# Squares of 32 by 32, loaded by DMA and turned by VectorE, in place of TensorE's transpositions with an identity

## The chip, the core and the metric

The kernel runs on one core of one Trainium2 chip. The metric is the device time of one execution in microseconds (us). The core has five engines that work side by side, each through its own list of instructions in order: TensorE (PE in the profile; PEld are its weight loads), VectorE (DVE), ScalarE (ACT), GpSimd (POOL) and SyncE (SP), which here only issues transfers. Transfers (DMAs) are issued by SP and by ScalarE and are carried out by 16 DMA engines. A DMA is cut into pieces that are contiguous in memory on both sides; the profile calls them packets.

## The reference, cut to what matters

Eight graphs (B = 8) of N = 2048 nodes with F = 256 features pass through two layers. Layer 0 is attention with 4 heads of 64 over chunks of 256 keys, each with a softmax of its own; layer 1 is graph attention with a score that is a sum of a source and a target term.

```python
# layer 0
q, k, v = (x @ W.T + b).reshape(B, N, 4, 64).transpose(0, 2, 1, 3)   # for Wq, Wk, Wv
scores = einsum('bhnd,bhjcd->bhnjc', q, kc) / 8       # keys in 8 chunks of 256
scores = where(mask == 0, -10, clip(scores, -10, 10))
attn = softmax(scores, axis=-1)                       # inside each chunk
ctx = einsum('bhnjc,bhjcd->bhnd', attn, vc)           # summed over the chunks
o = ctx.reshape(B, N, 256) @ Wo.T + bo + x
o = layernorm(o) * gamma + beta
x1 = layernorm(x + o)
# layer 1
Wh = x1 @ W1                                          # 4 heads of 64
e = leaky_relu(s_src[i] + s_dst[j], 0.2)              # s = einsum(Wh, a)
alpha = softmax(where(adj, e, -inf)); h = elu(alpha @ Wh)
out = layernorm(x1 + h)
```

A matrix product on TensorE contracts over the 128 partitions. So x, the contexts and x1, which come with nodes on the partitions, must be turned (features on the partitions) before they are multiplied with a weight matrix. That turning is what the change is about.

## The kernel before, in words

Everything is float32. The nodes of a graph are cut into four blocks of CH = 512 (index g or q); a block is QT = 4 tiles of 128 nodes. qT and kT hold queries and keys turned (128 features of a head pair by nodes, KC = 2 such halves); vaug holds the values with a column of ones, so that a product gives the softmax's sums too.

A graph's layer 0 is a loop over 64 slots (`for s in range(SLOTS)`, L837): four query blocks q, two head pairs hp, eight key chunks c; i = s % 16 is the slot's place within its query block. In a slot TensorE computes the scores of the next slot (`scores`, L335), VectorE clips and masks them (L346), ScalarE takes exponentials (L358), TensorE multiplies with the values (`product`, L368, in two halves k), ScalarE copies the result out of PSUM (L375), VectorE inverts the sums and GpSimd adds the chunk to the context (`normalize`, L383 to L392). Between the two halves of `product` stands a part of layer 1 of the graph before: three tiles, for each of which VectorE makes edge factors (L651) and TensorE multiplies (L671). In the first graph the masks are turned there instead (class `Masks`). So two graphs are always in work: layer 0 of b and layer 1 of b - 1.

Three things are turned by TensorE, as a product with an identity into PSUM, then copied to SBUF by ScalarE:

- x for the projections: `transposed` (L252), eight transpositions of 128 by 128 (L258) and a copy (L261). `project(b, g)` gives the pieces load, turn, keys, values, queries of a block.
- the contexts: `context(q, hp)` (L394), four transpositions (L399) and a copy into qT (L402), whose old queries are used up by then. It runs for hp = 0 at the end of slot 9 and for hp = 1 at the end of slot 1 of the next query block.
- x1: `Between.turn(c)` (L493), four transpositions (L498) and a copy (L501) for each half c. `Between` takes a finished query block through the output product (L466), residual, two norms, and the product with W1 (`values`, L514). Its steps are spread over the slots of the next query block by two tables: BESIDE (ahead of the slot's products, on VectorE) and BEHIND (after them).

Within each engine the order is the program's (`manual_schedule`); nothing is reordered. Transfers are issued by SP in program order too, each when what it waits for is done: masks for the clip three slots ahead (`load_slab`, L322), edges eight tiles ahead (L633), x blocks (L247). x1 is also kept in DRAM (x1D) for the residual of layer 1; the store goes to a list `outgoing` that SP works off at the top of a slot. Small buffers of a pool with one tag share its count of buffers: "xb" (two) serves x to be projected, x as residual and x1 as residual, "xT" (two) serves all turned blocks.

Between the slots of two graphs stands a list `order` (L910): the last query block's `Between`, whose x1 is turned by `transposed` (`turn_all`), the four projections of the next graph, and the factors of layer 1. After the last graph layer 1 runs alone.

Of the kernel before, what the change touches and what calls it, by code (L numbers as in the profile page):

```python
# [17 lines left out]
P = 128  # L18
CH = 512
# [3 lines left out]
def adj_resnorm_kernel(  # L23
# [37 lines left out]

    QS = HP * NK
# [45 lines left out]
    x1D = tc.dram_tile([B, NCH, P, QT, F], F32, name="x1D")  # L108
# [135 lines left out]

    def load_x(b, g, name):
        t = blocks.tile([P, QT, F], F32, tag="xb", name=name)
        nc.sync.dma_start(  # L247
            out=t, in_=x[b, g * CH : (g + 1) * CH, :].rearrange("(t p) f -> p t f", p=P)
        )
        return t  # L250

# [12 lines left out]
    def project(b, g):  # L264
# [4 lines left out]
        def load():  # L269
            st["x"] = load_x(b, g, "xp")  # L270

        def turn():
            st["xT"] = transposed(st["x"], "xT")
# [119 lines left out]

    def context(q, hp):  # L394

# [44 lines left out]
    class Between:  # L440
# [48 lines left out]
        def finish(self):  # L489
            self.b2.apply(self.y)  # L490
            outgoing.append(lambda: nc.sync.dma_start(out=x1D[self.b, self.g], in_=self.y))

        def turn(self, c):  # L493
            if c == 0:
                self.x1T = blocks.tile([P, KC, CH], F32, tag="xT", name="x1T")
            pt = psM.tile([P, CH], F32, tag="psM", name="pt")
            for k in range(QT):
                nc.tensor.transpose(  # L498
                    pt[:, k * P : (k + 1) * P], self.y[:, k, c * P : (c + 1) * P], identf
                )  # L500
            nc.scalar.copy(self.x1T[:, c, :], pt)  # L501
# [29 lines left out]

    BESIDE = {
        1: [lambda o: o.bias()],
        3: [lambda o: o.add((0, 1))],
        4: [lambda o: o.add((2, 3)), lambda o: o.a.stats((0, 1))],
        5: [lambda o: o.a.stats((2, 3)), lambda o: o.shift()],
        7: [lambda o: o.scale()],
        8: [lambda o: o.again(), lambda o: o.b2.stats((0, 1))],
        9: [lambda o: o.b2.stats((2, 3))],
    }  # L540
    BEHIND = {
        2: lambda o: o.output((0, 1)),
        3: lambda o: o.output((2, 3)),
        6: lambda o: o.a.apply(o.y),
        10: lambda o: o.finish(),
        11: lambda o: o.turn(0),
        12: lambda o: o.turn(1),
        13: lambda o: o.values((0,)),
        14: lambda o: o.values((1,)),
        15: lambda o: o.values((2,)),  # L550
    }

# [169 lines left out]
    class Close:  # L722


        def __init__(self, b, g):
# [3 lines left out]
            nc.sync.dma_start(out=self.x, in_=x1D[b, g])  # L729
# [5 lines left out]
        def finish(self):  # L735
            o = blocks.tile([P, QT, F], F32, tag="y", name="o")
            self.n.apply(o)
            rows = slice(self.g * CH, (self.g + 1) * CH)
            outgoing.append(
                lambda: nc.sync.dma_start(  # L740
                    out=out[self.b, rows, :].rearrange("(t p) f -> p t f", p=P), in_=o
                )
            )
# [77 lines left out]
    for b in range(B):  # L821
# [15 lines left out]
        for s in range(SLOTS):  # L837
# [5 lines left out]
            before = group  # L843
            if i == 0:
                group = Between(b, q - 1, sd, waug) if q else None
            if s:
                normalize(s - 1)
            if s + 1 < SLOTS:
                scores(s + 1)

            if group:
# [15 lines left out]
            if i == 0 and before:  # L867
                before.values((3,))
            if i == 1 and q:
                context(q - 1, 1)  # L870
            if i == QS // 2 + 1:
                context(q, 0)
# [33 lines left out]
        if b + 1 < B:  # L906
            (l0, t0, k0, v0, q0), (l1, t1, k1, v1, q1), (l2, t2, k2, v2, q2), (l3, t3, k3, v3, q3) = [
                project(b + 1, g) for g in range(NCH)
            ]
            order = [l0, begin, lambda: before.values((3,)), steps[0], t0, k0, ctx, l1, v0, steps[1]]  # L910
# [72 lines left out]
```

## Time and profile before

Three runs took 3926.72, 3927.82 and 3929.75 us. The profiled execution took 3929.08 us, with a span of 3927.3 us and a mean granted TensorE clock of 0.993.

| what | profile | where |
|---|---|---|
| turning x on TensorE | 256 transpositions, 34.1 us busy | L258 |
| turning contexts on TensorE | 256, 41.6 us busy | L399 |
| turning x1 on TensorE, in slots | 192, 31.5 us busy | L498 |
| turning x1 on TensorE, last block of a graph | 64, 9.6 us busy | L258 |
| copies behind them on ScalarE | 1012 ns for 1024 columns, 607 to 611 ns for 512 | L261, L402, L501 |
| scores, clip, exponentials in slots | 1022.7 us PE, 1192.6 us DVE, 1051.4 us ACT | L335, L346, L358 |
| products of layers 0 and 1 | 1159.6 and 1088.8 us PE | L368, L671 |
| edge factors | 1343.2 us DVE | L651 |

How to read it: "busy" is the time in which at least one instruction of a group ran, so matmuls that overlap are not counted twice, and the mean of one instruction (here about 275 ns for a transposition) is longer than its share of the busy time. In a line of the timeline the first number is the start in us, the second the length of a run of like instructions, then engine, line, operation, the tile written and those read, and the count; a bracket gives idle time ahead of it and what ended it. A view of waits or of one engine's timeline shows more of the limit than the shares do, because stages differ: the first graph has no layer 1 beside it, and the last layer 1 has no layer 0.

### The profile page before, as it was taken

The page shows a single profiled execution, that of the slowest core. Times are in us where ns is not written, and L with a number is a line of the kernel's source. Part 1 is how long each engine was busy: PE and PEld are TensorE (multiplying, and loading weights), DVE is VectorE, ACT ScalarE, POOL GpSimd, SP SyncE. Part 2 cuts the span into 40 slices and gives each one's busy share as a digit, 9 for nine tenths or more (in the row PEclk, how much of TensorE's full clock was granted, in tenths as well). Part 3 has the DMA queues.
Part 4 walks back from the last instruction along what each step waited for, and adds up shares of the span by engine and source line. Part 5 has one row for each costly group of instructions (what it writes and reads, how often), then busy time and mean ns, then how long its engine had stood idle before and what let it go on. Part 6 is the DMA issues. An engine that isn't in the chain of part 4 may idle for free. (4 is left out here: it accounts for less than half of the span.)

```text
span 3927.3 us, 160298 instructions
## 1 busy us (share of the span) xinstructions
PE 3781.5 (96%) x72740; PEld 2820.0 (72%) x72740; DVE 3115.4 (79%) x4698; ACT 2028.6 (52%) x3753; POOL 1388.4 (35%) x1202
## 2 busy tenths in 40 slices
PE   7998999999999999999999999999999999999787
PEld 4665677776777767776777767777677776776676
DVE  3776398885988769885898849888598876987798
ACT  4665445554555555555555545555455555555321
POOL 0444233332343333432443324433243333434310
PEclk9999999999999999999999999999999999999899
DMA  6641232222322233331432224322232323322244
GB/s 150 136 93 35 70 92 80 83 72 93 105 84 85 63 115 91 85 85 59 128 92 81 81 75 122 84 78 72 93 108 81 85 63 115 95 80 71 84 144 124
DMA packets 379259, 356.50 MB, mean 91 GB/s; under 512 B 87376, under 2 KB 335568, under 8 KB 378576
## 3 DMA queue, kind: packets, MB, share of 16 engines
q1 hardware_dynamic: 375040, 344.02, 30.5%
q8 instruction: 568, 9.31, 1.0%
q10 hardware_dynamic: 3536, 2.23, 0.2%
q14 instruction: 115, 0.94, 0.1%
HBM read 303.96 MB, written 42.21 MB: 88 GB/s over the span
## 5 line engine op out<-in xcount | busy, mean ns | idle before, releaser
L346 DVE SCALAR_TENSOR_TENSOR pr<-ps,slab 128x1024 f32<-128x1024 f32 x1024 | 1192.6, 1205 | 284.3 <-PE ps L335 283.5
L368 PEld LDWEIGHTS pc<-vaug,pr 128*64 128x64 f32 x32768 | 1041.1, 138 | 437.5 <-issue 248.4
L651 DVE SCALAR_TENSOR_TENSOR e<-srow,gd,et 128x640 f32<-128x640 f32 (+1 forms) x1536 | 1343.2, 930 | 6.2 <-PE pa L671 6.2
L368 PE MATMUL pc<-vaug,pr 128*64 128x65 f32 x32768 | 1159.6, 224 | 37.3 <-ACT raw L375 31.9
L358 ACT ACTIVATE pr<-pr 128x1024 f32<-128x1024 f32 x1024 | 1051.4, 1056 | 229.4 <-DVE pr L346 212.7
L671 PE MATMUL pa<-waug,e 128*64 128x65 f32 x32768 | 1088.8, 224 | 41.0 <-DVE e L651 37.5
L671 PEld LDWEIGHTS pa<-waug,e 128*64 128x64 f32 x32768 | 1023.4, 139 | 71.1 <-DVE e L651 37.4
L335 PE MATMUL ps<-qT,kT 64*128 64x512 f32 x4096 | 1022.7, 617 | 11.0 <-DVE pr L346 8.1
L390 POOL TENSOR_TENSOR part<-raw,rd 128x512 f32<-128x512 f32 x448 | 468.6, 1046 | 1442.3 <-DVE rd L383 1425.2
L375 ACT COPY raw<-pc 128x260 f32<-128x260 f32 x1024 | 382.1, 373 | 1129.2 <-PE pc L368 1111.9
L335 PEld LDWEIGHTS ps<-qT,kT 64*128 64x128 f32 x4096 | 352.7, 186 | 345.6 <-issue 223.4
L392 POOL TENSOR_TENSOR acc<-acc,part 128x512 f32<-128x512 f32 x448 | 574.2, 1282 | 35.2
L383 DVE RECIPROCAL rd<-raw 128x8 f32<-128x8 f32 x512 | 101.1, 197 | 172.5 <-ACT raw L375 165.6
L390 POOL TENSOR_TENSOR acc<-raw,rd 128x512 f32<-128x512 f32 x64 | 66.8, 1043 | 387.4 <-DVE rd L383 386.6
L699 ACT ACTIVATE hh<-pa,dn 128x64 f32<-128x64 f32 x512 | 114.2, 321 | 100.7 <-DVE dn L695 96.9
L514 PE MATMUL pw<-w_sb,x1T 128*128 128x264 f32 x512 | 141.3, 406 | 4.3 <-ACT sd L525 4.3
L279 PE MATMUL pp<-xT,wk_sb 128*128 128x512 f32 x256 | 120.1, 613 | 18.6 <-ACT xT L261 18.1
L426 POOL TENSOR_TENSOR rs_c<-rs_c,nhalf 128x4 f32<-128x4 f32 x32 | 55.6, 1737 | 226.8 <-DVE off_c L425 226.8
L466 PE MATMUL po<-wo_sb,qT 128*128 128x256 f32 x512 | 124.8, 389 | 0.0
L279 PE MATMUL pp<-xT,wq_sb 128*128 128x512 f32 x256 | 117.5, 602 | 5.5 <-DVE y L477 3.1
L295 PE MATMUL pv<-wv_sb,xT 128*128 128x256 f32 x512 | 115.9, 379 | 0.0
L426 POOL TENSOR_TENSOR rs_a<-rs_a,nhalf 128x4 f32<-128x4 f32 x32 | 56.3, 1761 | 153.2 <-DVE off_a L425 153.2
(93 smaller groups left out, 2050.7 us busy)
## 6 DMA issues: line engine op xcount, KB each, us to landing
et<-edgeD SPq DMA_DIRECT2D x256, 320.0 KB, 3.1
slab<-clipD SPq DMA_DIRECT2D x512, 128.0 KB, 3.4
et<-edgeD SPq DMA_DIRECT2D x128, 384.0 KB, 3.6
srow<-rowD SPq DMA_DIRECT2D x64, 320.0 KB, 4.4
xp<-in_x_dram SPq DMA_DIRECT2D x32, 512.0 KB, 4.5
xg<-in_x_dram SPq DMA_DIRECT2D x32, 512.0 KB, 4.9
x1D<-y SPq DMA_DIRECT2D x32, 512.0 KB, 3.0
x1g<-x1D SPq DMA_DIRECT2D x32, 512.0 KB, 5.5
```

The costliest lines, as they stand in the source:

```text
L279: nc.tensor.matmul(pp[:, c, :], lhsT=w[:, kc, c * P : (c + 1) * P], rhs=st["xT"][:, kc, :], start=(kc == 0), stop=(kc == KC - 1),)
L335: nc.tensor.matmul(ps[:, k, :], lhsT=kT[rows, hp, t * P : (t + 1) * P], rhs=qT[rows, hp, cols], start=True, stop=True,)
L346: nc.vector.scalar_tensor_tensor(pr, pss[u], -CLIP, slab[:, u, :].unsqueeze(1).to_broadcast([P, 2, CH]), op0=ALU.max, op1=ALU.min,)
L358: nc.scalar.activation(pr, pr, AF.Exp, scale=0.125)
L368: nc.tensor.matmul(pc[z * D : (z + 1) * D, i, :], lhsT=probs[s][u][:, k, i * P + z * D : i * P + (z + 1) * D], rhs=vaug[:, KT * c + u, 2 * ...
L375: nc.scalar.copy(raws[s][:, k], pc)
L390: nc.gpsimd.tensor_mul(part, raw[:, :, :, :D], rd.to_broadcast([P, 2, QT, D]))
L392: nc.gpsimd.tensor_add(accv, accv, part)
L466: nc.tensor.matmul(po[:, k, :], lhsT=qT[:, c, t * P : (t + 1) * P], rhs=wo_sb[:, c, :], start=(c == 0), stop=(c == KC - 1),)
L514: nc.tensor.matmul(pw[:, k, : F + 2 * H], lhsT=self.x1T[:, c, u * P : (u + 1) * P], rhs=w1_sb[:, c, :], start=(c == 0), stop=(c == KC - 1),)
L651: nc.vector.scalar_tensor_tensor(e[:, :w], self.rows[n][:, :w], self.gd[:, h, j : j + 1], self.edge[k // JG][:, j % JG, :w], op0=ALU.max, ...
L671: nc.tensor.matmul(self.pa[z * D : (z + 1) * D, i * D1 : (i + 1) * D1], lhsT=e[:, i * P + z * D : i * P + (z + 1) * D], rhs=self.waug[:, j ...
```

## The change

Each of the three is turned in another way, except the last query block of each graph, which is left as it was (its hp = 1 context and its x1).

A block that lies in DRAM with a node per row is loaded by `load_squares`: for each 32 features one DMA puts, for all groups of 32 nodes, node r of the group on partition a * 32 + r, and the 32 features of it (128 B) next to those of the other groups. So each square of 32 nodes by 32 features stands in its final place, but unturned. VectorE's transpose then turns every square of 32 by 32 in place of its grid, and the whole is turned. A block of x or x1 takes eight such DMAs with 512 pieces each and one VectorE instruction of 1024 columns; a context half takes four DMAs and 512 columns.

- x is in DRAM already. Block 0 of the next graph is now loaded at the top of slot 63, ahead of `order`; the turn of block 0 stands right behind `begin`.
- A context is first stored to a new DRAM array ctxD, by a DMA on ScalarE's queue at the end of slots 0 and 8 (`send_context`), is loaded at the top of slots 1 and 9, after the slab's load (`load_context`), and turned in slots 3 and 11, behind the clip (`turn_context`), straight into qT.
- x1 is stored, now as rows by node, on ScalarE's queue behind the last norm (slot 11); it is loaded back at the top of slot 12 and turned in slot 14. x1D's new layout also holds for the residual of layer 1.

The steps of `Between` move by a slot to the later side, and the four `values` pieces move to the ends of slots 14 and 15 and of slots 0 and 1 of the next query block (table AFTER). For the query block before the last, the second pair of `values` falls into `order`.

```diff
+    def load_squares(dst, src):
+        for c in range(src.shape[1] // P):
+            for a in range(P // SQ):
+                f0 = c * P + a * SQ
+                nc.sync.dma_start(
+                    out=dst[a * SQ : (a + 1) * SQ, c, :].rearrange("r (k s) -> r k s", s=SQ),
+                    in_=src[:, f0 : f0 + SQ].rearrange("(k r) s -> r k s", r=SQ),
+                )
+    def turned(t, name):
+        dst = blocks.tile([P, KC, CH], F32, tag="xT", name=name)
+        nc.vector.transpose(dst.rearrange("p c n -> p (c n)"), t.rearrange("p c n -> p (c n)"))
+        return dst
...
-            st["x"] = load_x(b, g, "xp")
+            st["x"] = load_turned(x, b, g, "xp")
-            st["xT"] = transposed(st["x"], "xT")
+            st["xT"] = turned(st["x"], "xT")
...
+    def send_context(b, q, hp):
+        acc = accs.pop((q, hp))
+        cols = slice(hp * P, (hp + 1) * P)
+        nc.scalar.dma_start(
+            out=by_node(ctxD, b, q)[:, :, cols], in_=acc.rearrange("p t k d -> p t (k d)")
+        )
+    def load_context(b, q, hp):
+        t = small.tile([P, 1, CH], F32, tag="ctx", name="ctx", bufs=1)
+        load_squares(t, ctxD[b, q * CH : (q + 1) * CH, hp * P : (hp + 1) * P])
+        sums[q, hp] = t
+    def turn_context(q, hp):
+        nc.vector.transpose(qT[:, hp, q * CH : (q + 1) * CH], sums.pop((q, hp))[:, 0, :])
...
-            outgoing.append(lambda: nc.sync.dma_start(out=x1D[self.b, self.g], in_=self.y))
+            nc.scalar.dma_start(out=by_node(x1D, self.b, self.g), in_=self.y)
+        def load(self):
+            self.t = load_turned(x1D, self.b, self.g, "x1t")
+        def turn(self):
+            self.x1T = turned(self.t, "x1T")
...
+    AHEAD = {12: lambda o: o.load()}
     BESIDE = {
         1: [lambda o: o.bias()],
-        3: [lambda o: o.add((0, 1))],
-        4: [lambda o: o.add((2, 3)), lambda o: o.a.stats((0, 1))],
-        5: [lambda o: o.a.stats((2, 3)), lambda o: o.shift()],
-        7: [lambda o: o.scale()],
-        8: [lambda o: o.again(), lambda o: o.b2.stats((0, 1))],
-        9: [lambda o: o.b2.stats((2, 3))],
+        4: [lambda o: o.add((0, 1))],
+        5: [lambda o: o.add((2, 3)), lambda o: o.a.stats((0, 1))],
+        6: [lambda o: o.a.stats((2, 3)), lambda o: o.shift()],
+        8: [lambda o: o.scale()],
+        9: [lambda o: o.again(), lambda o: o.b2.stats((0, 1))],
+        10: [lambda o: o.b2.stats((2, 3))],
+        14: [lambda o: o.turn()],
     }
     BEHIND = {
-        2: lambda o: o.output((0, 1)),
-        3: lambda o: o.output((2, 3)),
-        6: lambda o: o.a.apply(o.y),
-        10: lambda o: o.finish(),
-        11: lambda o: o.turn(0),
-        12: lambda o: o.turn(1),
-        13: lambda o: o.values((0,)),
-        14: lambda o: o.values((1,)),
-        15: lambda o: o.values((2,)),
+        3: lambda o: o.output((0, 1)),
+        4: lambda o: o.output((2, 3)),
+        7: lambda o: o.a.apply(o.y),
+        11: lambda o: o.finish(),
+        14: lambda o: o.values((0,)),
+        15: lambda o: o.values((1,)),
     }
+    AFTER = {0: lambda o: o.values((2,)), 1: lambda o: o.values((3,))}
...
+            if i == 1 and q:
+                load_context(b, q - 1, 1)
+            if i == QS // 2 + 1:
+                load_context(b, q, 0)
+            if group and i in AHEAD:
+                AHEAD[i](group)
+            if s == SLOTS - 1 and b + 1 < B:
+                turns = [project(b + 1, g) for g in range(NCH)]
+                turns[0].pop(0)()
...
-            order = [l0, begin, lambda: before.values((3,)), steps[0], t0, k0, ctx, l1, v0, steps[1]]
+            order = [begin, t0, lambda: before.values((2, 3)), steps[0], k0, ctx, l1, v0, steps[1]]
```

## The prediction

> **What bounds the kernel now**
>
> I read the engines' busy shares first, then the work in order of time inside single slots, then the groups by shape, and last the transfers. (The chain that ended last covers only the final microseconds here and says nothing about the rest.)
>
> ```profile
> PE 3781.5 (96%) x72740; PEld 2820.0 (72%) x72740; DVE 3115.4 (79%) x4698; ACT 2028.6 (52%) x3753; POOL 1388.4 (35%) x1202
> ```
>
> A busy PE need not be the bound, so I take two neighbouring slots of the second batch (TensorE, in order of time; start, length):
>
> ```profile
> 629.79 1.99 PE L335 MATMUL ps<-qT,kT 64*128 64x512 f32 x8
> 631.71 1.15 PE L368 MATMUL pc<-vaug,pr 128*64 128x65 f32 x32
> 632.69 1.92 PE L671 MATMUL pa<-waug,e 128*64 128x65 f32 x60
> 634.44 1.10 PE L368 MATMUL pc<-vaug,pr 128*64 128x65 f32 x32
> 635.48 1.99 PE L335 MATMUL ps<-qT,kT 64*128 64x512 f32 x8
> ...
> 640.12 1.10 PE L368 MATMUL pc<-vaug,pr 128*64 128x65 f32 x32
> 641.16 0.66 PE L399 MATMUL pt<-identf,acc 128*128 128x128 f32 x4
> 641.75 1.99 PE L335 MATMUL ps<-qT,kT 64*128 64x512 f32 x8
> ```
>
> Without extras a slot takes 635.48 - 629.79 = 5.69 us; with one context's four transposes 641.75 - 635.48 = 6.27 us, and no wait stands between. TensorE sets the slot, and four transposes cost it 0.58 us.
>
> VectorE is the next limit. The same stretch on it:
>
> ```profile
> 632.26 2.30 DVE L346 SCALAR_TENSOR_TENSOR pr<-ps,slab 128x1024 f32<-128x1024 f32 x2
> 634.48 1.48 DVE L486 TENSOR_TENSOR y<-y,xg 128x1024 f32<-128x1024 f32 x1
> 636.00 0.75 DVE L416 BATCH_NORM_STATS2 st_b<-y 128x6 f32<-128x256 f32 x2
> 639.37 2.31 DVE L346 SCALAR_TENSOR_TENSOR pr<-ps,slab 128x1024 f32<-128x1024 f32 x2
> ```
>
> Undisturbed, the clip (L346) starts 1.18 us after the slot's scores begin (607.77 after 606.59). Here it starts at 639.37 instead of 635.48 + 1.18, so VectorE runs 2.7 us behind. One group later this lag reaches 3.0 us, and the slot takes 6.50 us instead of 6.27. A lag of 2.8 us is therefore about what the slots absorb.
>
> Between two batches TensorE also waits for the copy out of PSUM that each transposition needs:
>
> ```profile
> 883.64 1.04 PE L258 MATMUL pt<-identf,xp 128*128 128x128 f32 x8
> 885.78 3.70 PE L279 MATMUL pp<-xT,wk_sb 128*128 128x512 f32 x8 [1.10 <-ACT xT L261]
> 896.66 1.04 PE L258 MATMUL pt<-identf,xp 128*128 128x128 f32 x8
> 898.14 0.70 PE L279 MATMUL pp<-xT,wq_sb 128*128 128x512 f32 x1 [0.44 <-DVE y L477]
> ```
>
> [...]
>
> - [...] row L451 has 1214 ns. I price a turn alike: estimate 1.2 us for 1024 columns, 0.65 us for 512.
> - [...]
> - [...] The new loads move pieces of 128 B.
>
> The trace can price such a piece. From 30 to 75 us, where masks are stored in 128 B pieces, the transfers show:
>
> ```profile
> DMA packets 19792, 7.72 MB, mean 172 GB/s; under 512 B 17014, under 2 KB 18175, under 8 KB 19789
> q1 hardware_dynamic: 19789, 7.68, 80.1%
> ```
>
> 0.801 x 45 us x 16 engines / 19789 is 29 ns per packet over all. Taking off the 2775 large ones, estimated at 50 ns (1161 of 1 KB; the page's mean on q1 is 0.305 x 3927 x 16 / 375040 = 51 ns) and 150 ns (1614, by their bytes), leaves 277 us for 17014: 16 ns. But these are stores; small loads from scattered DRAM rows are not shown. Bounds: 7 ns (128 of the mean 917 B at 51 ns) and 51 ns (a piece costs a mean packet). I take 15 ns.
>
> **The change part by part, against the profiled span of 3927.3 us**
>
> *Contexts and x1 inside slots.* A batch has seven contexts in slots (0, 0; then two each for q = 1, 2, 3, less the last, which stays on TensorE) and six x1 half blocks (three groups of two). Each takes 0.59 us of TensorE: row L399 gives 41.6 us / 256 x 4 = 0.65, less overlap. So 13 x 0.59 = 7.7 us per batch, 61 us in eight. The first batch has no second-layer work but shows the same 0.58 (394.17, 399.43). Projected values only move a slot later; one more of them falls between batches and one less into a slot: nothing. ScalarE loses its copies, which were off the path.
>
> *What VectorE pays.* It gains 2 x 0.65 + 1.2 = 2.5 us per group of 16 slots. Measured start to start, its own slot is 4.7 us, 0.98 under TensorE's 5.68. The added values reach slot 14 (turn of x1), where TensorE has 6.77 us: hidden. The turn in slot 3 stands beside an output product (7.6 us): hidden. The turn in slot 11 does not stand in such company. The norm's steps are one slot later, and slots 9 to 12 have lost transposes that gave VectorE time. Lag, slot by slot: 0.5 at slot 6; 7.3 us of work, 2.15 at slot 7; 1.2; 1.6; again, statistics and L707 (7.6 us), 3.5 at slot 10. That is 0.7 beyond 2.8, then 0.2 at 11 and 0.1 at 12: 1.0 us of stall, against 0.3 now. Loss 0.7 us per group, 21 groups with a second layer beside them: 15 us.
>
> *The transfers.* A context is stored from ScalarE's queue at the end of slots 0 and 8, its squares are loaded in the next slot, and needed two slots after that: 15.8 us after the load's slot begins, against about 2.5 (store) + 1.6 (four issues) + 3 = 7. Hidden. For x1 it is tight. Now the apply runs to 3.9 us after its next slot's start (1581.40 + 2.08 against 1579.57). Add the store, 4.1 us (as for the output, which has the new layout):
>
> ```profile
> out_dram<-o SPq DMA_DIRECT2D x32, 512.0 KB, 4.1
> clipD<-clip SPq DMA_DIRECT2D x32, 80.0 KB, 2.0
> xp<-in_x_dram SPq DMA_DIRECT2D x32, 512.0 KB, 4.5
> ```
>
> so loads start 8.0 us into slot 12. They are eight issues of 0.39 us (the median of today's x issue, which also has 512 pieces) with 256 pieces per engine: the larger of 3.1 and 256 x 15 ns = 3.8, plus 2.2 to land, 6.0 us. x1T is needed by TensorE at 3 x 5.68 = 17.0, less 1.2 for the turn: 15.8. Ready at 14.0, so 1.8 us spare. SP stands still meanwhile until slot 12 + 11 us. Behind it are slabs (three slots ahead) and edge chunks (eight tiles, 15 us ahead), so nothing starves. ScalarE's queue waits at a store for GpSimd's sum, which ends about 2.3 us into the slot, earlier than the copy ahead of the store, and for the eighth transfer before it in the program (eight completion counters go round), which is some slots old; the exponentials behind it are not held. On VectorE, the edge factors (L651) and the next clip stand behind a turn, so a late load reaches TensorE through both. In the first batch slots are 4.7 us and the spare vanishes: loss 1 us.
>
> *Between batches*, seven times. x0 is loaded a slot ahead and turned while TensorE does other work: 1.04 + 1.10 = 2.1 us. Turn 3: 1.04. Turns 1 and 2 go too (1.48 + 1.27), but TensorE then meets the norm of the last group: 16.3 us from the end of its output product (896.7 to 913.0), with 14.5 us of products left in front of the turn instead of 17.3. Gain there 1.0. Sum 4.1 us, 29 us in seven. The next x waits only for VectorE's turn, 7 us to load against 12 us between turns.
>
> *Start.* The first product waits until 15.67 us for ScalarE, which is held by weight loads. VectorE turns x at about 11: 4 us gained. The phase's transfers go from 80% towards 95%, so I keep 4.
>
> Sum: 61 - 15 - 1 + 29 + 4 = 78 us, 3849 on the profiled span; its run took 3929.1 and the others 3926.7 to 3929.8, so 3849 for the median.
>
> **Rivals**
>
> *VectorE takes it back.* If it absorbs no more than now, each group in slots loses its gain of 2.4 us rather than 0.7: another 21 x 1.7 = 36 us, 3885. For: VectorE's share in 490 to 866 us is 337.5 / 376 = 90%. Against: slots 13 to 3 show no lag, and the larger turn lies there. A turn at double price adds 0.65 at slot 11, 14 us.
>
> *x1's load is late.* At 30 ns a piece the load takes 2.5 + 7.7 = 10.2 us, ready at 18.2, 2.4 late, in 24 groups: 58 us less gain, 3907.
>
> *Slower.* The same place at 51 ns: 2.5 + 13.1 = 15.6 us, 7.8 late, 187 us, so 4036. The gain is gone when each of the 24 loads is 78 / 24 = 3.3 us late, at 34 ns a piece. For: unmeasured scattered reads. Against: 16 ns for the stores.
>
> *The transposes were hidden anyway.* Then no change; the slot above speaks against it (6.27 to 5.69).
>
> **How the numbers follow**
>
> Main case 0.66 (3815 to 3875: from no added stall, no loss at the norm, up to double-price turns); VectorE 0.14 (3885); late load 0.08 (3907); slower 0.09; no change 0.03. The range 3815 to 3893 holds the first two. 0.2% is about what the runs can tell apart. Faster 0.88, same 0.03, slower 0.09.
>
> **What would show it**
>
> Slots with a context at 5.7 us, not 6.27; no wait of TensorE between first turn and L279; VectorE's transposes at 1.2 and 0.65 us; a clip lag up to 3.5 us at slot 10. Wrong, if VectorE waits for x1t or ctx transfers in slots 14, 3 or 11, if TensorE waits for x1T, or if TensorE's slots stay as long although the transposes are gone.

## The result, and the profile after

The changed kernel takes 3890.01 us, median of 4 runs (3888.07 to 3892.72); the kernel before, on the same chip, 3928.49 us (3926.72 to 3929.75). The ratio is 0.9903, 95% interval 0.9886 to 0.992. It is faster by 38.5 us, half of the 79 us forecast. The profiled execution spans 3888.7 us against 3927.3 us, 38.6 us less, so the two traces can be compared directly.

The first line of the page that answers to the one shown of before:

```profile
PE 3696.5 (95%) x72068; PEld 2752.5 (71%) x72068; DVE 3204.7 (82%) x4810; ACT 1946.2 (50%) x3601; POOL 1384.4 (36%) x1202
```

TensorE lost 85 us of busy time and 672 instructions, VectorE gained 89 us. But the span fell by only 39 us: TensorE now waits more. The view of TensorE's waits names where (total us, how often, longest), first of after, then of before:

```profile
PE pc L393 <- ACT raw L400: 63.1, 104, 2.3
```

```profile
PE pc L368 <- ACT raw L375: 31.9, 56, 1.9
```

The attention product (`product`, L393) waits for ScalarE's copy of the product before it out of PSUM (`raw`, L400). This wait doubled, although ScalarE's own load fell. Of the added 31 us, 21.7 lie in slots 8 and 13 of the second to fourth groups of 16 slots (in batches with a second layer), where the kernel before has none of these waits, and 6.2 in slot 13 of the first group.

To see what it is, here are two neighbouring slots of the second batch, in order of time (start, length, and in brackets a wait with its releaser). TensorE, from slot 12 of a group to slot 14:

```profile
747.59 1.99 PE L360 MATMUL ps<-qT,kT 64*128 64x512 f32 x8
...
753.55 1.99 PE L360 MATMUL ps<-qT,kT 64*128 64x512 f32 x8
756.22 1.15 PE L393 MATMUL pc<-vaug,pr 128*64 128x65 f32 x32 [0.68 <-ACT raw L400]
...
759.98 1.99 PE L360 MATMUL ps<-qT,kT 64*128 64x512 f32 x8
```

VectorE and ScalarE at the same time:

```profile
751.49 2.30 DVE L371 SCALAR_TENSOR_TENSOR pr<-ps,slab 128x1024 f32<-128x1024 f32 x2
```

```profile
752.69 2.19 ACT L383 ACTIVATE pr<-pr 128x1024 f32<-128x1024 f32 x2 [0.28 <-DVE pr L371]
754.79 1.11 ACT L737 ACTIVATE hh<-pa,dn 128x64 f32<-128x64 f32 x5
755.77 0.40 ACT L400 COPY raw<-pc 128x260 f32<-128x260 f32 x1
```

Read them from the bottom. TensorE could have started L393 at 755.54 and starts at 756.22, when the copy of `raw` is done. The copy was ready to go when the second product of slot 12 ended, but ScalarE works in order: the exponentials came first, and after them `hh`, five activations of the second layer's tail, 1.11 us. The exponentials were late because the clip (L371) started at 751.49, which is 751.49 - 747.59 - 1.18 = 2.72 us behind. Slot 13 takes 759.98 - 753.55 = 6.43 us instead of 5.68. The lag alone, 2.72 us, is within the 2.8 us that the forecast allowed. With `hh` in its way it is not.

Between two batches, VectorE and then TensorE, at the second gap and (last line) at the third:

```profile
874.97 0.49 DVE L745 SCALAR_TENSOR_TENSOR h<-ee,hp 128x320 f32<-128x320 f32 x1 [2.50 <-ACT hp L743]
875.38 1.24 DVE L274 STREAM_TRANSPOSE xT<-xp 128x1024 f32<-128x1024 f32 x1
```

```profile
876.67 5.40 PE L304 MATMUL pp<-xT,wk_sb 128*128 128x512 f32 x8 [2.32 <-DVE xT L274]
...
1339.29 3.70 PE L304 MATMUL pp<-xT,wk_sb 128*128 128x512 f32 x8 [2.32 <-DVE xT L274]
```

VectorE had x0 in SBUF and nothing else to do, yet its turn starts at 875.38: in program order it stands behind L745, the end of the last tail, and that waits for ScalarE. TensorE waits 2.32 us, twice the 1.10 us of before. In the second gap the same eight products then take 5.40 us instead of 3.70; the granted clock was 0.77 from 877 to 879 us and 0.58 from 879 to 882 us.

The transfers, which the forecast doubted most, from the page and from the lists of single instructions (min/median/max ns):

```profile
xp<-in_x_dram SPq DMA_DIRECT2D x256, 64.0 KB, 2.3
```

```profile
L435 DVE STREAM_TRANSPOSE qT<-ctx x56: 695/702/707, 138.5 to 3604.1; 128x512 f32<-128x512 f32 x56
```

A transfer of 64 KB, sixteen squares, lands in 2.3 us. In the trace's record of single packets one of 128 B takes 12.9 ns of a transfer engine in the mean (409,600 of them); in the kernel before, where the 65,536 packets of this size are all stores, it takes 12.9 ns too. The lists show no wait of VectorE for a context or for x1 in the slots with a second layer.

**Where the 38.6 us are.** I took the start of every slot's scores from the trace. A gap is the time from the last scores of a batch to the first of the next. One product of projected values, 6.77 - 5.68 = 1.09 us, moved per batch from the slots into the gap (in the last batch, into the end); the third column has it put back.

| part | measured | without the moved product | forecast |
|---|---|---|---|
| slots, 8 batches | 3084.3 to 3055.0: -29.3 | -20.6 | -61 + 16 = -45 |
| gaps, 7 | 495.6 to 486.7: -9.0 | -16.6 | -29 |
| start | +0.3 | +0.3 | -4 |
| end | -0.6 | -1.7 | 0 |
| sum | -38.6 | -38.6 | -78 |

So 24 us are missing in the slots, 12 in the gaps and 4 at the start.

### The profile page after: what moved, and what is told of

Same layout as the page of the kernel before. It is cut to its first block, busy times and chain, and to the rows that moved or that the text cites. A ratio compares the mean times of both kernels' runs of the same rounds, so it can differ in the third digit from the quotient of the medians.

```text
span 3888.7 us, 160154 instructions
## 1 busy us (share of the span) xinstructions
PE 3696.5 (95%) x72068; PEld 2752.5 (71%) x72068; DVE 3204.7 (82%) x4810; ACT 1946.2 (50%) x3601; POOL 1384.4 (36%) x1202
## 5 line engine op out<-in xcount | busy, mean ns | idle before, releaser
L371 DVE SCALAR_TENSOR_TENSOR pr<-ps,slab 128x1024 f32<-128x1024 f32 x1024 | 1192.7, 1205 | 237.3 <-PE ps L360 234.0
L393 PEld LDWEIGHTS pc<-vaug,pr 128*64 128x64 f32 x32768 | 1041.6, 138 | 475.3 <-ACT raw L400 243.9
L393 PE MATMUL pc<-vaug,pr 128*64 128x65 f32 x32768 | 1161.4, 224 | 68.9 <-ACT raw L400 63.1
L709 PE MATMUL pa<-waug,e 128*64 128x65 f32 x32768 | 1089.8, 224 | 41.0 <-DVE e L689 39.2
L709 PEld LDWEIGHTS pa<-waug,e 128*64 128x64 f32 x32768 | 1025.2, 139 | 70.3 <-DVE e L689 39.8
L415 POOL TENSOR_TENSOR part<-raw,rd 128x512 f32<-128x512 f32 x448 | 467.9, 1044 | 1472.7 <-DVE rd L408 1460.1
L400 ACT COPY raw<-pc 128x260 f32<-128x260 f32 x1024 | 383.5, 375 | 1139.0 <-PE pc L393 1092.4
L417 POOL TENSOR_TENSOR acc<-acc,part 128x512 f32<-128x512 f32 x448 | 574.0, 1281 | 35.2
L415 POOL TENSOR_TENSOR acc<-raw,rd 128x512 f32<-128x512 f32 x64 | 66.8, 1043 | 366.1 <-DVE rd L408 365.3
L304 PEld LDWEIGHTS pp<-xT,wk_sb 128*128 128x128 f32 x256 | 48.3, 198 | 106.5 <-issue 49.6
```

What stands on the lines that cost most here:

```text
L304: nc.tensor.matmul(pp[:, c, :], lhsT=w[:, kc, c * P : (c + 1) * P], rhs=st["xT"][:, kc, :], start=(kc == 0), stop=(kc == KC - 1),)
L371: nc.vector.scalar_tensor_tensor(pr, pss[u], -CLIP, slab[:, u, :].unsqueeze(1).to_broadcast([P, 2, CH]), op0=ALU.max, op1=ALU.min,)
L393: nc.tensor.matmul(pc[z * D : (z + 1) * D, i, :], lhsT=probs[s][u][:, k, i * P + z * D : i * P + (z + 1) * D], rhs=vaug[:, KT * c + u, 2 * ...
L400: nc.scalar.copy(raws[s][:, k], pc)
L415: nc.gpsimd.tensor_mul(part, raw[:, :, :, :D], rd.to_broadcast([P, 2, QT, D]))
L417: nc.gpsimd.tensor_add(accv, accv, part)
```

## The experiments

Theory A: VectorE's lag makes the exponentials late, and where ScalarE has a tail (or a norm's apply) between them and the copy of `raw`, a smaller lag than 2.8 us already stops TensorE; in the gaps the turn of x0 stands behind L745. Rivals: T, the transfers took the rest; V, VectorE's lag or the added turns by themselves did; S, the steps between the layers came one slot later, and that alone did; W, a later tail helps any such kernel. The table gives a group of 16 slots (the third of a batch, mean of seven batches): length of the slot, and in brackets by how much the clip lags in it, in us.

| slot | before | after | e7 | e2 | e10 | e13 |
|---|---|---|---|---|---|---|
| 7 | 5.68 (1.16) | 5.68 (2.12) | 5.68 (2.12) | 5.68 (2.12) | 5.68 (1.86) | 5.68 (1.86) |
| 8 | 5.68 (1.63) | 6.12 (1.34) | 6.12 (1.34) | 6.12 (1.35) | 5.68 (1.16) | 5.69 (1.16) |
| 9 | 6.51 (3.05) | 5.68 (1.36) | 5.68 (1.37) | 5.68 (1.37) | 5.68 (1.62) | 5.68 (1.62) |
| 10 | 5.68 (2.81) | 5.78 (2.91) | 5.79 (2.92) | 5.79 (2.91) | 5.68 (2.77) | 5.68 (2.77) |
| 11 | 6.37 (2.00) | 5.87 (3.00) | 5.87 (3.00) | 5.87 (3.00) | 6.22 (3.36) | 6.23 (3.36) |
| 12 | 6.27 (0.61) | 5.95 (2.72) | 5.95 (2.11) | 5.96 (2.12) | 5.95 (2.45) | 5.95 (2.01) |
| 13 | 6.77 (0) | 6.44 (1.75) | 5.87 (1.16) | 5.88 (1.20) | 5.68 (1.48) | 5.68 (1.03) |
| all 16 | 101.82 | 100.88 | 100.31 | 100.33 | 99.94 | 99.95 |

In the kernels before and after, `hh` stands in slots 7, 12 and 1. A late clip in one slot shows in the length of the next, by way of ScalarE.

VectorE's lag has a second way to TensorE, in the same slot and without ScalarE: the edge factors stand ahead of the clip on VectorE, and TensorE's products of layer 1 (L671 before, L709 after) wait for them. What a slot loses this way is its own lag less 2.81 us. In before that is 3.05 - 2.81 = 0.24 us in slot 9, in after 0.10 and 0.19 us in slots 10 and 11 (lags 2.91 and 3.00), in e10 0.54 us in slot 11 (3.36). So the 2.8 us of the forecast hold for this way, and here V is right. Of the 1.77 us that TensorE waits in this group of after, 0.29 come by it, and 1.20 (slots 8 and 13) by the way of theory A.

### e1: the tail behind the second product

```diff
-                    lower.step()
+                    lower.tiles()
             product(s, 1)
+            if lower and (b + 1 < B or s < SLOTS - LATE):
+                lower.rest(1)
```

> The changed kernel, with one step of the second layer's tail (dn, hh, ee and hp, h) issued behind the slot's second product instead of ahead of its layer-1 products. Theory A (a late clip makes the exponentials late, and in slots in which ScalarE has the five activations of hh, 1.11 us, between the exponentials and the copy of raw, TensorE waits for that copy): in groups with a second layer 0.9 us of stall less per group of 16 slots, 21 groups, 15 to 20 us less: about 3872. TensorE's wait for raw falls from 63 us to about 45. Rival T (the missing gain went to the transfers) and rival V (VectorE's lag reaches TensorE through the clip itself): no change, 3890.

3902.9 us (ratio to the kernel before 0.9935, 0.9922 to 0.9949): 13 us slower than after, a miss of the number. The slots explain it. Slots 8 and 13 lost their stalls, as theory A says (6.12 to 5.68, 6.44 to 5.68). But slot 12 grew from 5.95 to 7.28 us and slot 10 from 5.78 to 6.24. ScalarE in slots 11 and 12:

```profile
746.02 1.14 ACT L737 ACTIVATE hh<-pa,dn 128x64 f32<-128x64 f32 x5
747.02 2.09 ACT L473 ACTIVATE y<-y,off_b,rs_b 128x256 f32<-128x256 f32 x4
...
749.60 0.38 ACT L400 COPY raw<-pc 128x260 f32<-128x260 f32 x1 [0.49 <-ACT y L473]
```

`hh` now meets the norm's apply (L473): 3.2 us in front of the next copy, and TensorE waits 0.96 us for it. Slot 10 loses its time the other way, by the edge factors: VectorE's part of the tail moved too, its lag there is 3.37 us, and 3.37 - 2.81 are the 0.56 us lost. The gaps took the rest: a lower clock fell on them more often. The edit moved the collision instead of taking it away; for slots 8, 12 and 13 it does show that a place on ScalarE decides, and no amount of work.

### e2: the first-half context turned in slot 15

```diff
-            if i == QS // 2 + 3:
+            if i == QS - 1:
                 turn_context(q, 0)
```

> The changed kernel, with the turn of a first-half context in slot 15 of the group instead of slot 11. Theory A: VectorE's lag in slots 11 to 13 is 0.65 us smaller there, the stall at slot 13 (0.76 us) mostly goes, and slot 15 has TensorE work enough to hide the turn: 0.4 to 0.5 us per group in 21 groups, about 10 us: 3880. Rival T (transfers): 3890. Rival S (only the shift of the norm's steps by one slot counts, the turns are hidden): 3890.

3883.8 us (0.9886, 0.9873 to 0.99). The slots fell from 3055.0 to 3041.3 us in sum, by 13.7, more than expected: the lag of slot 12 fell from 2.72 to 2.12, and slot 13 from 6.44 to 5.88. Only 6 us arrived, because the gaps rose: the first product after the wait took the longer time, 5.40 us, in all of the six gaps after the first (one of six in after).

### e3: x0 turned in the last slot

```diff
-            if s == SLOTS - 1 and b + 1 < B:
+            if s == SLOTS - 2 and b + 1 < B:
...
+        if b + 1 < B:
+            turns[0].pop(0)()
         normalize(SLOTS - 1)
```

> The changed kernel, with the first x block of the next batch loaded in the last slot but one and turned on VectorE in the last slot, ahead of the second layer's last step (which waits for ScalarE). Theory A: TensorE's wait of 2.32 us in front of the first product after a batch goes, seven times: 16 us, 3874. Rival Q (TensorE then stands at the next wait, for ScalarE's evacuation of qT): 1 us or less each, 3883 to 3890.

3873.8 us (0.9861, 0.9848 to 0.9874), as theory A says. VectorE, then TensorE, at the second gap:

```profile
868.15 1.19 DVE L274 STREAM_TRANSPOSE xT<-xp 128x1024 f32<-128x1024 f32 x1
...
874.61 0.49 DVE L745 SCALAR_TENSOR_TENSOR h<-ee,hp 128x320 f32<-128x320 f32 x1 [2.51 <-ACT hp L743]
```

```profile
873.82 3.60 PE L304 MATMUL pp<-xT,wk_sb 128*128 128x512 f32 x8
```

L745 still waits its 2.5 us, but nothing stands behind it. TensorE's wait is gone, its products are at 3.60 us, and six gaps take 66.9 us instead of 69.45 or 71.16. The slots stay (3055.6 us).

### e4: only the shift by one slot; e6: the transfers added to it

e4 is the kernel before with the tables of steps of the changed kernel (`add` in 4 and 5, apply in 7, `finish` in 11, transpositions in 12 and 13, values from 14); e6 adds to e4 the stores and the loads of squares:

```diff
+            if i == 1 and q:
+                load_context(b, q - 1, 1)
+            if i == QS // 2 + 1:
+                load_context(b, q, 0)
+            if group and i == 12:
+                group.load()
...
+                send_context(b, q - 1, 1)
```

> The kernel before, with the steps between the layers one slot later as in the changed kernel, and all of TensorE's transpositions kept. Theory A: the peak of VectorE's lag moves towards the slot of hh, but the transpositions still give VectorE time, so 0 to 0.4 us per group: 3928 to 3937. Rival S (the shift by one slot alone cost what is missing in the slots): about 25 us more than before, 3953. Rivals T and V: 3928.

> The kernel before with its steps one slot later (the run e4), and with the stores of contexts and x1 and the loads of their squares of the changed kernel added; what is loaded is not used, TensorE's transpositions are kept. Theory A: the transfers cost nothing: 3937, as e4. Rival T: they slow the slabs, the edges or SP's queue: 3950 to 3965.

The line of e4's waits that the next sentences use:

```profile
PE pt L399 <- ACT sd L525: 9.7, 16, 0.9
```

e4: 3937.3 us (1.0022, 1.0014 to 1.0031), 8.9 us more than before. With the moved product put back the slots cost 16 us more and the gaps 6 less. Of the 16, 9.7 are a wait of this kernel alone, which the changed one can't have (a context's transposition in slot 1 waits for the PSUM buffer of the moved values), so S leaves about 6 of the 24 us missing in the slots. But it shows how: slot 8 is already 6.13 us here, after a lag of 2.12 in slot 7. The shift put that lag onto `hh`. e6: 3942.2 us (1.0033, 1.0021 to 1.0046), 4.8 more than e4: the slots cost 1.1 more in all eight batches, each gap 0.55. Rival T falls for the slots. In the gaps it isn't the transfers but an issue: ScalarE now issues x1's store (0.37 us) between the norm's apply and the copy of a turned x block. In e6, at the fourth gap:

```profile
1851.70 1.01 ACT L283 COPY xT<-pt 128x1024 f32<-128x1024 f32 x1 [0.44 <-ACT y L464]
```

In e4 this copy follows the apply without a pause, and TensorE waits 0.45 us for it instead of 0.98. In seven gaps that is 3.8 of the 4.8 us. The changed kernel has this issue at the same place.

### e7: no turns of contexts and x1

```diff
-        nc.vector.transpose(qT[:, hp, q * CH : (q + 1) * CH], sums.pop((q, hp))[:, 0, :])
+        sums.pop((q, hp))
...
-            self.x1T = turned(self.t, "x1T")
+            self.x1T = self.t
```

> The changed kernel without VectorE's turns of contexts and x1 (the squares are loaded straight to where the turned block would stand, so these products see blocks that are not turned; x is still turned). Theory A: VectorE's lag peaks fall by 0.65 to 1.2 us per group, the stalls in slots 8 to 13 nearly go (8 keeps its 0.4): 1.0 to 1.3 us per group, 3863 to 3870. Rival T: the transfers hold TensorE, so nothing changes: 3890.

3886.1 us (0.9891, 0.9877 to 0.9904); slots 3044.3 us, 10.7 less than after, the rest again lost in the gaps. The table carries the point: e7 (100.31) and e2 (100.33) agree. Leaving out all three turns of a group is worth no more than moving the one in slot 11. The turns in slots 3 and 14 cost nothing, as forecast, and slots 8 and 10 to 12 keep their stalls without any turn: V in the form "the turns did it" is too small.

### e8: x by TensorE, contexts and x1 by squares

```diff
-            st["x"] = load_turned(x, b, g, "xp")
+            st["x"] = load_x(b, g, "xp")
...
-            st["xT"] = turned(st["x"], "xT")
+            st["xT"] = transposed(st["x"], "xT")
```

> The changed kernel with x loaded by node and transposed on TensorE as before; contexts and x1 stay with the squares. Theory A: the gaps between batches go back to those of e4 less nothing else, 71.3 us against 69.5 (or 71.2 where the clock falls): 3895 to 3905; the start stays as it is. Rival Q (the turns of x in the gaps gain nothing, since the wait for VectorE and the lower clock take it all): 3890.

3900.2 us (0.9928, 0.9914 to 0.9941): the squares of x are worth 10 us of the 38.5, in the gaps (71.3 us each). The first scores come 0.9 us earlier than in after: at the start the squares cost a little.

### e5: three moves, with the steps one slot earlier again

```diff
-    AHEAD = {12: lambda o: o.load()}
+    AHEAD = {11: lambda o: o.load()}
-        14: [lambda o: o.turn()],
+        13: [lambda o: o.turn()],
-            if i == 3 and q:
+            if i == 2 and q:
                 turn_context(q - 1, 1)
```

(all other steps of the tables a slot earlier too, with the edits of e2 and e3)

> The changed kernel with three moves: the steps between the layers one slot earlier again (the second-half context turned in slot 2, output products behind 2 and 3, x1 loaded in 11 and turned in 13), the first-half context turned in slot 15, and x0 turned in the last slot. Theory A: the squares cost nothing but where VectorE's lag meets ScalarE's tail, so the gains add: 14 us in the slots (the turn in 15, without what the gap took back), 16 to 18 us in the gaps, 9 us from the shift: 3890 - 40 = 3850, near the forecast. Rival T: with a slot less between store and turn, VectorE waits for the context's squares in slot 2 and stalls TensorE: 3870 or more, with a wait of VectorE for ctx in the profile.

3868.7 us (0.9845, 0.9832 to 0.9858), short of 3850. VectorE waits 1.4 us in all for a context's squares, so T isn't why. The slots sum to 3045.8 us, 8.7 of them the product that came back: 4 better than e2, not 9. With the steps back, slots 9 and 10 took 5.92 and 6.27 us at lags of 3.05 and 3.40; the kernel before has a context's transpositions in slot 9, in which VectorE catches up. In three gaps the third x block met the lower clock.

### e9: one norm step on GpSimd

```diff
         def shift(self):
             row = beta_sb.unsqueeze(1).to_broadcast([P, QT, F])
-            nc.vector.tensor_add(self.r, self.r, row)
+            nc.gpsimd.tensor_add(self.r, self.r, row)
```

> The changed kernel with one norm step (the addition of beta to the residual, 128x1024, in slot 6) on GpSimd instead of VectorE. Theory A: VectorE's lag falls by 1.2 us from slot 7 on, and the stalls in slots 8 to 13 (1.78 us per group) fall by 1.0 to 1.3 us in 21 groups: 21 to 27 us, 3863 to 3869. Rival C (the stalls are ScalarE's own and not VectorE's lag): 3890. A loss would be GpSimd's slower addition holding the norm in the gaps.

3897.2 us (0.9919, 0.9906 to 0.9933), 7 slower than after: a miss. The first half came true: the lag of slot 7 fell from 2.12 to 0.99, and slot 8 went back to 5.68 us. But then the lag grew to 3.93 in slot 10, which took 6.80 us (3.93 - 2.81 = 1.12 more than 5.68). GpSimd and VectorE (the third line gives single durations, min/median/max ns) from slot 7 on:

```profile
716.12 3.02 POOL L497 TENSOR_TENSOR xg<-xg,beta_sb 128x1024 f32<-128x1024 f32 x1
719.10 1.05 POOL L415 TENSOR_TENSOR part<-raw,rd 128x512 f32<-128x512 f32 x1
720.23 1.73 POOL L417 TENSOR_TENSOR acc<-acc,part 128x512 f32<-128x512 f32 x1
```

```profile
719.16 4.28 DVE L689 SCALAR_TENSOR_TENSOR e<-srow,gd,et 128x640 f32<-128x640 f32 x3
```

```profile
L689 DVE SCALAR_TENSOR_TENSOR e<-srow,gd,et x2: 1669/1778/1887, 719.2 to 720.7; 128x640 f32<-128x640 f32 x2
```

Three edge factors take 4.28 us here and 2.44 elsewhere. The addition (3.02 us on GpSimd, 1.22 on VectorE) pushed GpSimd's L415 and L417 from the time of the clip into that of the edge factors. The first of them starts just after L415 does and ends 0.7 us after it; the second starts at 720.7, inside L417, and ends at 722.6, again 0.7 us after L417's end (721.96). Undisturbed, one takes 0.87. The trace of after has the same on a smaller scale: of the edge factors of this shape the 950 with no L415 or L417 beside them take 0.88 us in the mean, the 60 with 0.3 to 0.6 us of them 1.07, and the two with more 1.62. The clip (L371) shows no such delay there: 1.20 us in the mean for the 825 with 0.6 us or more of L415 and L417 beside them, 1.22 for the 122 with none. What makes the difference between edge factors and clip was not shown.

### e10: every tail one slot later; e14: the same in the kernel before

```diff
+            yield 1
             dn = small.tile([P, n, 1], F32, tag="dn", name="dn")
...
-            lower.rest(4)
+            lower.rest(5)
```

> The changed kernel with every tail of the second layer one slot later (dn in 7, 12 and 1, hh in 8, 13 and 2), nothing else moved. Theory A: hh leaves the slots that follow the lag peaks, so the 0.45 us in slot 8 and the 0.76 us in slot 13 shrink to 0.2 in sum, part of it comes back in slots 9 to 12: 0.3 to 0.7 us per group less, 3875 to 3884. Rival V (lag alone counts, whatever ScalarE has there): 3890.

> The kernel before, with every tail one slot later and nothing else changed. Theory A: before the change the lag peaks (3.0 us in slot 9, 2.8 in 10) were over when hh came (slots 12 and 7), the stall per group was 0.33 us, so there is nothing to gain, and hh in 8 and 13 meets lags of 1.6 and 0: 3925 to 3930. Rival W (a later tail helps any kernel of this kind, so that e10's gain says nothing of the change): 3910 to 3917.

e10: 3878.2 us (0.9872, 0.9858 to 0.9885); the slots fall by 17.0 to 3038.0 us. Slots 8 and 13 are back at 5.68, part of it returned in slot 11 by the edge factors. The tail's steps on VectorE moved too, so the lags of slots 7 and 12 fell to 1.86 and 2.45 us; with `hh` still behind them they would have cost about 0.2 and 0.5 us (estimate from after, where 2.12 cost 0.44 and 2.72 cost 0.76), so the place of `hh` is a little over half of what these two slots gained. Four of six gaps met the lower clock, hence 12 us in all.

e14: 3946.4 us (1.0043, 1.0029 to 1.0057), 17 us slower than before: a miss of the number, on the far side of W. The two waits for `raw`, of e10 and of e14:

```profile
PE pc L393 <- ACT raw L400: 44.8, 70, 2.3
```

```profile
PE pc L368 <- ACT raw L375: 49.1, 102, 1.9
```

The same edit takes the wait from 63.1 to 44.8 us in the changed kernel and raises it from 31.9 to 49.1 in the kernel before. So a later tail doesn't help as such, and W falls. But the wait for `raw` isn't what makes e14 slow. `hh` came into slot 8, where the lag is 2.17, and slot 9 went from 6.51 to 7.06 us; the last step of the tail on VectorE (0.5 us) also moved, from slot 3, which has 7.61 us, to slot 4, which has 5.68, and VectorE's lag in slot 9 rose from 3.05 to 3.61 us. The edge factors and TensorE's products with them in slot 9, in before and then in e14:

```profile
1204.43 2.44 DVE L651 SCALAR_TENSOR_TENSOR e<-srow,gd,et 128x640 f32<-128x640 f32 x3
1205.57 2.16 PE L671 MATMUL pa<-waug,e 128*64 128x65 f32 x60
```

```profile
1208.73 2.44 DVE L651 SCALAR_TENSOR_TENSOR e<-srow,gd,et 128x640 f32<-128x640 f32 x3
1209.81 2.22 PE L671 MATMUL pa<-waug,e 128*64 128x65 f32 x60
```

The products end 0.86 us after the edge factors in both. TensorE's wait of 0.41 us for `raw` ahead of them is hidden in that, and 3.61 - 2.81 = 0.80 us is what slot 9 takes beyond its 6.27. Of the 0.69 us that e14 adds to this group, 0.55 are V's way (slot 9) and 0.24 theory A's (slot 10); slot 11 gives 0.10 back. So e14 speaks against W and not against V. The case for theory A rests on after itself, where a lag of 2.12 us with `hh` behind it costs 0.44 us and one of 3.00 us without `hh` 0.10 us of TensorE's wait for `raw` (slot 12), and on e2 and e10.

### e11, e12, e13: the moves together

e11 is e2 and e3 together. e12 adds to it e9's addition on GpSimd and issues the squares of the very first block ahead of the weights. e13 is e11 with the later tail of e10.

> The changed kernel with the first-half context turned in slot 15 and x0 turned in the last slot of the batch before (the steps between the layers stay one slot later). The two act in different places, so the gains add: 13.7 us in slots (seen in e2), 7 x 2.57 us in gaps (seen in e3): 3890 - 32 = 3858. If the gaps fall into the lower clock again: 3870.

> The two moves of e11, the addition of beta on GpSimd, and the squares of the very first x block issued ahead of the weights in the program. Theory A: e11's 3858, less 0.8 to 1.1 us per group in 21 groups (17 to 23 us), less 3 to 7 us at the start: 3828 to 3838. Rival C: only the start gains, 3853.

> The changed kernel with the two moves of e11 and the tails one slot later of e10. Theory A: the stalls of slot 13 are taken away by both, so the gains in slots add only in part: 17 us (seen in e10) and 3 to 9 of the 14 us (seen in e2), with 18 us in the gaps: 3890 - 38 to 44 = 3846 to 3852. Rival: the two undo each other in the slots (the turn in 15 meets a tail in 13 to 1), 3858 or more.

e11: 3859.5 us (0.9824, 0.981 to 0.9837), as expected: the gains add, and with no wait in front of the first product the six gaps after the first are 66.87 us.

e12: 3860.9 us (0.9828, 0.9815 to 0.9841), no gain over e11. GpSimd's addition cost 6 us in the slots (7.6 in e9), and gave 5 back in the gaps. The start didn't move. What SyncE waited for in the first 13 us of e12 (total us, how often, longest):

```profile
SPq L137 <- DMA wv_sb<-in_wvT_dram: 4.0, 1, 4.0
SPq L137 <- DMA xp<-in_x_dram: 2.2, 1, 2.2
```

The eight issues still take 11.5 us (11.3 in after). Of these 8.0 us are waits, the two shown and 1.8 for `bo_sb` (4.2, 2.3 and 1.4 in after). In the traces the transfers of SyncE and ScalarE count on eight semaphores in turn (in after 4016 to 4032 counts on each), and an issue waits until the transfer that used its semaphore before has landed: in after `wv_sb` lands at 6.36 us and the next issue on its semaphore, the fourth of x, starts at 6.37; `bo_sb` lands at 8.60, and the issue of x behind it starts at 8.62. So the fourth issue of x waits for the weights `wv_sb`. Moving the issues ahead of the weights in the program changed nothing, because both traces deal the semaphores out in the same order: wk_sb, x, bk_sb, wv_sb, x, wq_sb, bq_sb, x, and round again.

e13: 3854.9 us (3850.7 to 3858.6; 0.9811, 0.9798 to 0.9824), the fastest of all: 35 us below the changed kernel. Its slots sum to 3036.5 us, hardly less than e10's 3038.0: the turn in 15 and the later tail take away the same stall of slot 13. Its group of 16 slots takes 99.95 us; the forecast, 101.82 - 4 x 0.59 + 0.7, was 100.16.

## Why the prediction was wrong in size

- *TensorE sets the slot, four transpositions cost 0.58 us*: right. Slot 9 went from 6.51 to 5.68 us.
- *VectorE's turns at 1.2 and 0.65 us, those in slots 14 and 3 hidden*: right (1.24 and 0.70 us; e7 against e2). The trace of before has no VectorE turn, so both prices were the author's estimates; that trace has 1214 ns for an addition of 1024 columns (L451) and 681 ns for one of 512 (L477).
- *Transfers hidden, 15 ns a piece*: right, 13 ns, for the stores too, which the forecast put at 16; no late x1 in the slots with a second layer, and in the first batch 2.5 us of TensorE's waiting for x1T (1 forecast for the whole batch). ScalarE's issue of x1's store, 0.37 us, was priced at nothing: it costs about 0.5 us per gap (e6), and part of slot 12, which takes 0.27 us more in after, e2, e7, e10 and e13 alike, with the issue between the norm's apply and a copy of `raw`.
- *"A lag of 2.8 us is therefore about what the slots absorb"*: this is the step that failed in the slots. It was read in slots 9 and 10, where TensorE's wait comes by the edge factors and ScalarE has no tail, and used for all. For the edge factors it is right: slots 10 and 11 lost 0.29 us, less than the 0.9 forecast, because the peak of the lag was 3.0 and not 3.5. The other lag was forecast well: 2.15 in slot 7 (2.12 measured). What the step lacked is the copy of `raw` behind `hh`. There only about 1.7 us are allowed, roughly 2.8 less the 1.11 us of `hh`: a lag of 2.12 in slot 7 cost 0.44 us, which puts the allowance at 1.7, and 2.72 in slot 12 cost 0.76, at 1.96 (1.7 again, if the 0.27 us by which slot 12 is longer are taken off the lag). The forecast had 0 and 0.1 there. In this group TensorE waits 1.77 us instead of 0.33, 1.4 more where the forecast had 0.7. The second group of a batch lost more (it gained 1.49 us where 4 x 0.59 + 1.09 = 3.45 were removed), and the first, with the output of an earlier batch beside it, about 0.7, which the forecast didn't count: in its slot 13 the lag reached 3.3 us. In seven batches that is about 5.4 us each against 2.1, in the first batch 3.3 against 1.
- *The gaps, 4.1 us each*: three of the four blocks came as forecast. From the first to the second block's product 0.07 and from there to the third 0.75 were gained (forecast 1.0 together), to the fourth 1.26 (1.04). The first gained 1.09 - 0.43 = 0.66 instead of 2.1: "turned while TensorE does other work" overlooked L745 ahead of the turn on VectorE, which waits for ScalarE. That is 10 of the 12 missing us; e3, which turns x0 ahead of L745, gave them back. One lower clock cost 1.7 more.
- *The start, 4 us*: failed. VectorE turned x at 15.0 us, not at 11: the first block's eight transfers took 11.3 us to issue, 7.9 of them waits for transfers that used the same counters. The forecast named these eight counters for the stores in the slots and left them out here.
- Of the rivals, "VectorE takes it back" (3885) came nearest in size and in place. Its reason, that VectorE absorbs no more than now, was only half of it: e10 left the amount of VectorE's work as it was and gave 17 us of the slots back. The measured 3890 lies in the stated range because that reached up to this rival. The ends of the main case, 3815 and 3875, don't follow from the terms named there: no added stall and no loss at the norm make 3849 - 15 - 12 = 3822, a turn at double price 3849 + 14 = 3863.

## What to carry to other kernels

Slack is not one number for a loop: read a tolerated lag in each slot, and subtract what the in-order engine behind it has between the late work and what frees the next buffer. When a change moves the steps by a slot, lay the peaks of the lag over the fixed work of every other engine; here moving a tail by one slot was worth 17 us in one direction in one kernel and in the other direction in the other, the first on ScalarE, the second mostly on VectorE. A wait in a list of waits need not be what sets the time: in e14 a later one hid it (0.41 us in slot 9). In after VectorE stood idle for 2.50 us with the turn of x0 ready behind L745: look for what waits in front, above all where one stage hands over to the next.

## What the runs showed that was not expected

- After a wait of 2.32 us, TensorE's next eight products took 5.40 us instead of 3.70 in some gaps and not in others: in 1 of 6 gaps in after, 6 of 6 in e2, 4 of 6 in e10. Where the wait was 1.10 us (before) or none (e3, e11, e13), these products never did. In the traces all changes of the granted clock lie on one grid of 3.413 us; a window here is one step of it. In after, e1, e2, e7, e9 and e10 there are 36 such gaps (without the first of each), all with a wait of 2.32 to 2.34 us: where at least 1.97 us of the wait fell into one window, the next window ran at a granted clock of 0.50 (21 gaps), and where at most 1.93 us did, it didn't (15 gaps). The second gap of after had 1.99 us in the window before this one (time, length, TensorE's busy time and instructions, granted clock, then the share and rate of the transfers):

```profile
878.09:881.51 3.42, 3.42 (x6) 0.50 0.76 120
```

Half of 3.42 us is 1.71, and the eight products lost 1.70. This describes these gaps and is no rule: in three gaps of e5 the third block lost it behind a wait of 0.94 us. An edit elsewhere shifts the gaps on this grid; in e2 they took back 5.4 of the 13.7 us that the slots gained in the profiled execution. So compare slots and gaps apart.
- A 128x1024 addition takes 2.79 us in the mean on GpSimd (e9) and 1.22 us on VectorE, and beside the work that it pushed aside two of VectorE's edge factors took 1.67 and 1.89 us instead of 0.87.
- A packet of 128 B took 12.9 ns of one transfer engine in the mean, in before, where all are stores, and in after, where most are loads.
- Transfers of two engines share eight counters of completion here, so a load of many small transfers can stand behind a load of weights on another queue (4.2 us behind `wv_sb` in after, 4.0 in e12).
